# Output weights and bias centred on ScalarE, gamma applied by column groups, two plain loads on GpSimd's queue

## The chip, the cores and the metric

The kernel runs on one core of one Trainium2 chip. The metric is the device time of one launch in microseconds. The median of three runs of the kernel before is 727.76 us (727.09 to 733.88).

## The reference

The program is two graph networks behind each other on the same 384 nodes with 1024 features and 12,672 edges, each as a residual: `x = x + net(relu(layernorm(x)))`. The first is attention with an edge mask. The second is a relational graph convolution of two layers, 768 wide, with six relations and four basis matrices. Cut to what matters here:

```python
# second network, h is relu(layernorm(x)), 384 x 1024
x = relu(h @ w_in + b_in)                       # 384 x 768
for l in range(2):
    h_in = x
    W = einsum('rb,bio->rio', comp[l], basis[l])
    h_all = einsum('ni,rio->rno', x, W)
    counts = zeros((6, n)).at[edge_type, dst].add(1.0)
    msg = h_all[edge_type, src] / counts[edge_type, dst][:, None]
    agg = segment_sum(msg, dst, num_segments=n)
    x = relu(agg + x @ root[l] + conv_bias[l]) + h_in
    x = batchnorm(x, bn_gamma[l], bn_beta[l])
h_final = x @ w_out + b_out                     # 384 x 1024
out = ln_gamma * (h_final - mean) / sqrt(var + eps) + ln_beta   # mean, var over the 1024
```

The mean over the 1024 columns of `x @ w_out + b_out` is `x` times the row means of `w_out` plus the mean of `b_out`. If each row of `w_out` and `b_out` has its mean taken away, the product has mean zero.

## The kernel before, in words

Nodes or features lie on the 128 partitions; 384 nodes are three tiles. All products are in float32, and most large ones are made with seven partial products instead of eight (the functions that add and subtract quarters of an operand make the terms for this).

**The relation tables.** The edges are not followed one by one. GpSimd scatters edge counts into two tables in device memory, `atab[0]` and `atab[1]`, with 99 indirect transfers that add (`put_count`, line 269), in turns between the two tables; each waits for the one before it on the same table. The tables together give, for each relation, a 384 x 384 matrix of counts. When the scatters are done, the matrix of relation r is read into the tile `A[:, r]`: first a plain load of its part of table 1, then, from GpSimd's queue, a load of its part of table 0 that adds on arrival (line 836, `accum_op`). For relations 0 and 1 the plain load stands on SyncE's queue (line 834), for the other four on GpSimd's (line 838). `add_up` (lines 339 and 340, GpSimd) adds the three node tiles of a relation, `share` (line 345) sums over the partitions with a matmul against ones into a bank called `ps_cnt`, ScalarE and VectorE make one over the count from it (348 to 350), and VectorE scales the matrix (351). `mix` (330 and 332) then weighs the six relations into four matrices, one for each basis, in the tile `At`.

**The convolution.** For each layer the code runs over the four bases b. Each has three weight loads of 768 KB (`wload`, line 80, on SyncE's queue, from a pool of five buffers), products of the node features with the basis into `H` (lines 969 and 963, banks `ps_g`), and sums of weights on VectorE (911, 913, 919). The dictionary `between` puts the shares and mixes at fixed places between these products: share 0 after the first third of basis 2 of layer 0, share 1 after the second, share 2 after the last, share 3 and the first mix behind basis 2, shares 4 and 5 in basis 3, the other mixes behind basis 3. Then come the root product (1003) and the products of `At` with `H` (`times`, line 1061, banks `ps_c`), in three pairs of feature blocks o0 and o1. For each block VectorE adds a bank to `XN` (`take`, line 1091), ScalarE rectifies (`rectify`, 1094), VectorE adds the input and takes statistics (`measure`, 1026 to 1032), ScalarE takes a square root (1033), and VectorE scales (`normalise_layer`, 1038 to 1042). ScalarE has first put the root product with its bias into `XN` (`begin`, 1047).

**The output.** After the last layer the output weights stand in three tiles of [128, 2, 1024]. For each node tile TensorE makes the product (1167), VectorE adds the bias `rowsB[:, 0]` (1171), takes statistics by 256 columns (1173), joins them (145), adds epsilon (147), ScalarE takes the root (148), VectorE takes the mean away and multiplies by gamma `rowsB[:, 1]` in two halves (1178), takes the reciprocal (1179) and multiplies, adding `x_sb` (1181), and SyncE and ScalarE store the halves (1182). The last tile is cut in three groups of columns, 512, 256 and 256.

**What sets the order.** All engines around the change run in the order of the program's text: the schedule is manual for TensorE, GpSimd, SyncE and VectorE from the start and for ScalarE from the second projection on. An engine runs its instructions in that order and waits on semaphores, and a queue whose next transfer waits holds back those behind it.

Of the kernel before, what the change touches and what calls it, by code (L numbers as in the profile page):

```python
# [10 lines left out]
F32 = mybir.dt.float32  # L11
# [3 lines left out]
AF = mybir.ActivationFunctionType  # L15
ALU = mybir.AluOpType

P = 128
# [4 lines left out]
D = 1024  # L23
# [9 lines left out]
L = 2  # L33
# [18 lines left out]
def gnn_kernel(ctx: ExitStack, tc: tile.TileContext, out, x, edges, chunks, cols, rows, small,  # L52
               wq, wk, wv, wiq, wik, wiv, wo, w_in, basis, root, w_out):
    nc = tc.nc
# [7 lines left out]
    tiny = ctx.enter_context(tc.tile_pool(name="tiny", bufs=4))  # L62
# [4 lines left out]
    def bank(i, name):  # L67
        return psum.tile([P, 512], F32, tag=f"bank{i}", name=name)

    def next_bank(name, among=range(8)):  # L70

        i = next(i for i in ring if i in among)
        ring.remove(i)
        ring.append(i)
        return bank(i, name)

    def wload(src, name):

        w = wpool.tile([P, *src.shape[1:]], F32, tag="w", name=name)
        nc.sync.dma_start(w, src)  # L80
        return w
# [60 lines left out]
    def row_spread(st):  # L142

        mv = tiny.tile([P, 2], F32, tag="mv", name="mv")
        nc.vector.bn_aggr(mv, st.rearrange("p a b -> p (a b)"))
        sd = tiny.tile([P, 1], F32, tag="sd", name="sd")
        nc.vector.tensor_scalar(sd, mv[:, 1:2], LN_EPS, None, ALU.add)
        nc.scalar.activation(sd, sd, AF.Sqrt)
        return mv, sd
# [173 lines left out]
    A = None  # L323
# [32 lines left out]
    with ExitStack() as inner:  # L356
# [263 lines left out]
        A = late.tile([P, R, NT, N], F32, tag="A", name="A")  # L620
# [5 lines left out]
        scale = 1.0 / math.sqrt(HD)  # L626
# [164 lines left out]
        for half in range(2):  # L791
            T1, T2, T3, T4 = OT[half]
            pa, pb, pc, pd = [next_bank("ps_y", range(1, 8) if half else range(1, 7))[:, :256] for _ in range(4)]
            c0, c1 = half * 512, half * 512 + 256
# [36 lines left out]
        tabs = [tab[:ACELLS, :].rearrange("(t p r d) o -> r p t (d o)", p=P, r=R, t=NT) for tab in atab]  # L831

        for r in range(2):
            nc.sync.dma_start(A[:, r], tabs[1][r])
        for r in range(R):
            nc.gpsimd.dma_start(A[:, r], tabs[0][r], accum_op=ALU.add)
            for n in {1: (2, 3), 2: (4,), 3: (5,)}.get(r, ()):
# [52 lines left out]
    with tc.tile_pool(name="conv", bufs=1) as cp:  # L890
# [33 lines left out]
        def load_basis(l, b):  # L924
            w = w_first.pop(0) if w_first else []
            return w + [wload(basis[l, b, part], "w_c") for part in range(len(w), 3)]
# [20 lines left out]
        w = load_basis(0, 0)  # L947
        T = weight_sums(w)
        for l in range(L):
# [3 lines left out]
            for b in range(B):  # L953
# [6 lines left out]
                def times(ps, x, y, start=False):  # L960

                    for c in range(3):
                        nc.tensor.matmul(ps, x[:, c], y(c), start=start and c == 0, stop=(c == 2),  # L963
                                         skip_group_check=not start)
# [27 lines left out]
                if b + 1 < B:  # L992
                    w = load_basis(l, b + 1)
# [4 lines left out]
            w = [wload(root[l, part], "w_c") for part in range(3)]  # L998
# [11 lines left out]
            if l + 1 < L:  # L1010
# [4 lines left out]
                w = load_basis(l + 1, 0)  # L1015
            else:
# [3 lines left out]
                rowsB = room[:, :3 * D].rearrange("p (j d) -> p j d", j=3)  # L1020
# [15 lines left out]
            def normalise_layer(o, mv, sc):  # L1036
                c = l * KC + o
                nc.vector.reciprocal(sc[:, 0:1], sc[:, 0:1])
                nc.vector.tensor_tensor(sc[:, 1:2], sc[:, 0:1], cols_sb[:, GAM + c:GAM + c + 1], ALU.mult)
                nc.vector.tensor_tensor(sc[:, 2:3], mv[:, 0:1], sc[:, 1:2], ALU.mult)  # L1040
                nc.vector.tensor_tensor(sc[:, 2:3], cols_sb[:, BET + c:BET + c + 1], sc[:, 2:3], ALU.subtract)
                nc.vector.tensor_scalar(XN[:, o, :], XN[:, o, :], sc[:, 1:2], sc[:, 2:3], ALU.mult, ALU.add)

            def begin(o):

                c = l * KC + o
                nc.scalar.activation(XN[:, o, :], pr[o], AF.Identity, bias=cols_sb[:, CB + c:CB + c + 1])  # L1047
# [7 lines left out]
            def q(i, j):  # L1055

                return At.rearrange("p b n d -> p (b n) d")[:, i * 6:i * 6 + 6, j * HN:(j + 1) * HN]

            def times(ps, x, y, start=False, stop=True):
                for c in range(6):  # L1060
                    nc.tensor.matmul(ps, x[:, c], y[:, c], start=start and c == 0, stop=stop and c == 5,  # L1061
                                     skip_group_check=True)

            T1, T2 = [room2[:, i * 1152:(i + 1) * 1152].rearrange("p (c d) -> p c d", c=6) for i in range(2)]
            T4 = keep.tile([P, 6, HN], F32, tag="mask8", name="T4")
            nc.vector.tensor_tensor(T1, q(0, 1), q(0, 0), ALU.subtract)
# [6 lines left out]
            def feature_sums(p):  # L1073

                s0, s1, s3 = spaces[p % 2 * 3:][:3]
                o0, o1 = 2 * p, 2 * p + 1
                S.append((s0, s1, h(o1, 0), s3))
                for dst, x, y, op in ((s0, h(o1, 0), h(o1, 1), ALU.add), (s1, s0, h(o0, 0), ALU.subtract),
                                      (h(o1, 0), h(o0, 0), h(o1, 0), ALU.subtract),
                                      (s3, h(o0, 1), s1, ALU.subtract)):  # L1080
                    nc.vector.tensor_tensor(dst, x, y, op)
                    yield
# [6 lines left out]
            def take(o, j, ps):  # L1089
                dst = XN[:, o, j * HN:(j + 1) * HN]  # L1090
                nc.vector.tensor_tensor(dst, dst, ps, ALU.add)  # L1091
# [13 lines left out]
            for o in range(KC):  # L1105
                begin(o)
            take(0, 0, pa)
            ready = None
            for p in range(pairs):
                last = p == pairs - 1  # L1110
                sums = iter(()) if last else feature_sums(p + 1)
                o0, o1 = 2 * p, 2 * p + 1
                pc = next_bank("ps_c")[:, :HN]
                times(pc, S[p][0], T1, True)
                take(o1, 1, pc)
                if ready:
                    normalise_layer(*ready)
                next(sums, None)
                times(pa, S[p][1], T2)
                take(o0, 1, pa)  # L1120
                next(sums, None)
                times(pc, S[p][3], q(1, 1))
                take(o0, 1, pc)
                ready = measure(rectify(o0))
                if last:

                    pd = next_bank("ps_c")[:, :HN]
                    times(pd, h(o1, 1), T4, True)
                    normalise_layer(*ready)
                    take(o1, 0, pd)  # L1130
                    times(pa, S[p][2], T3)
                    take(o1, 1, pa)
                    take(o1, 0, pa)
                    normalise_layer(*measure(rectify(o1)))
                    continue
                times(pa, S[p][2], T3)
                take(o1, 1, pa)
                normalise_layer(*ready)
                for _ in sums:
                    pass  # L1140
                following = first_of(p + 1)
                times(pa, h(o1, 1), T4)
                take(o1, 0, pa)
                take(o1 + 1, 0, following)
                ready = measure(rectify(o1))
                pa = following
# [5 lines left out]

        for t in range(NT):
            nc.gpsimd.tensor_tensor(x_sb[:, t, :], x_sb[:, t, :], rowsB[:, 2, :], ALU.add)  # L1154
        w = [wload(w_out[part], "w_out") for part in range(3)]
        hf_ = cp.tile([P, NT, D], F32, tag="H", name="hf")
        for t in range(NT):
            hf = hf_[:, t, :]
            last = t == NT - 1
            ps = [next_bank("ps_f") for _ in range(3 if last else 2)]  # L1160

            parts = [(ps[0], 0, 512), (ps[1][:, :256], 512, 768), (ps[2][:, :256], 768, D)] if last else \
                [(ps[0], 0, 512), (ps[1], 512, D)]
            for ks in ((range(4), range(4, KC)) if t == 0 else (range(KC),)):
                for p, c0, c1 in parts:
                    for k in ks:
                        nc.tensor.matmul(p, XT[:, k, t * P:(t + 1) * P], w[k // 2][:, k % 2, c0:c1],  # L1167
                                         start=(k == 0), stop=(k == KC - 1))
            st = tiny.tile([P, 4, 6], F32, tag="st", name="st")
            for p, c0, c1 in parts:  # L1170
                nc.vector.tensor_tensor(hf[:, c0:c1], p, rowsB[:, 0, c0:c1], ALU.add)
                for c in range(c0, c1, 256):
                    nc.vector.bn_stats(st[:, c // 256, :], hf[:, c:c + 256])
            mv, sd = row_spread(st)

            parts = ((nc.sync, slice(0, 512)), (nc.scalar, slice(512, D)))
            for _, cs in parts:
                nc.vector.scalar_tensor_tensor(hf[:, cs], hf[:, cs], mv[:, 0:1], rowsB[:, 1, cs], ALU.subtract, ALU.mult)
            nc.vector.reciprocal(sd, sd)
            for queue, cs in parts:  # L1180
                nc.vector.scalar_tensor_tensor(hf[:, cs], hf[:, cs], sd, x_sb[:, t, cs], ALU.mult, ALU.add)
                queue.dma_start(out[t * P:(t + 1) * P, cs], hf[:, cs])
# [62 lines left out]
```

## Time and profile before

| | |
|---|---|
| median of three runs | 727.76 us |
| the profiled execution | 729.8 us, its span 728.0 us |
| TensorE busy | 700.2 us (96%) |
| VectorE busy | 515.0 us (71%) |
| GpSimd busy | 307.7 us (42%) |
| ScalarE busy | 157.7 us (22%) |
| mean granted TensorE clock | 0.991 |
| scatters into the count tables, line 269 | 99, 164.4 us busy |
| weight loads of a basis | 24 of 768 KB, 5.4 us from issue to landing in the median |
| relation loads on SyncE's queue, line 834 | 2 of 576 KB, 4.1 and 5.2 us to landing |
| relation loads on GpSimd's queue, lines 836 and 838 | 10 of 576 KB, 11.1 us to landing in the median |

All durations in the profile come from one execution, and the span is counted from the first instruction to the last. A line of a group gives busy time, the mean of one in nanoseconds, and the idle time before it with what ended it. In the timeline the first number is the start, the second the duration, and a bracket tells how long the engine had stood idle before and who released it. TensorE shows two records for each float32 matmul, so a group of six matmuls is x12.

### The profile page before, as it was taken

The numbers are of one execution on the slowest core, as the hardware profiler recorded it, in microseconds if no ns is written. First come the engines' busy times: TensorE is split into PE (matmuls) and PEld (weight loads), VectorE is DVE, ScalarE is ACT, GpSimd is POOL, SyncE is SP. The second block draws the span as 40 slices with busy tenths as digits, with TensorE's granted clock in tenths as the row PEclk, the third lists the DMA queues.
The fourth block names the chain that finished last, engine by engine and source line by source line (L and its number), as shares of the span: only waits on it lengthen the run. The fifth ranks groups of instructions, "written<-read, shape, count | busy, mean of one in ns | idle before, by whom it ended". The sixth has DMA issues, their size and how long they took to land.

```text
span 728.0 us, 8835 instructions
## 1 busy us (share of the span) xinstructions
PE 700.2 (96%) x3228; PEld 526.4 (72%) x3228; DVE 515.0 (71%) x1307; ACT 157.7 (22%) x360; POOL 307.7 (42%) x237
## 2 busy tenths in 40 slices
PE   7999999999999999999998499999999999999995
PEld 7759999999985444588965255557975555579943
DVE  6877696969877799777342179799878676506756
ACT  4201111111113577201310115201131111001100
POOL 1366677777575787586888454000000000030000
PEclk9999999999999999999999799999999999999999
DMA  8797787265426323525112997221103213700001
GB/s 300 261 364 206 235 248 216 43 218 198 126 71 207 84 3 61 169 33 131 1 2 0 251 319 208 85 89 44 43 1 131 76 59 125 277 27 1 1 29 58
DMA packets 40536, 91.00 MB, mean 125 GB/s; under 512 B 19644, under 2 KB 27680, under 8 KB 36270
## 3 DMA queue, kind: packets, MB, share of 16 engines
q1 hardware_dynamic: 18478, 79.62, 30.7%
q0 software_dynamic: 21008, 8.42, 10.1%
q10 hardware_dynamic: 1008, 2.41, 1.0%
q8 instruction: 25, 0.41, 0.2%
q14 instruction: 17, 0.14, 0.1%
HBM read 79.27 MB, written 11.16 MB: 124 GB/s over the span
## 4 chain that ended last, share of the span: by engine, by line
PE 60%; POOL 15%; DMA 10%; DVE 7%; issue 5%; ACT 1%; SPq 0%; DVEq 0%; POOLq 0%; ACTq 0%
POOL atab L269 14%; PE ps_k L386 10%; PE ps_g L969 10%; PE ps_c L1061 9%; PE ps_g L963 9%; DMA atab<-count,at 7%; PE ps_q L404 6%; PE ps_q L386 5%; PE ps_f L1167 4%; DVE At L332 4%; PE ps_v L386 4%; PE ps_c L1003 3%; DMA mtab<-m_val,at 2%; DMA w_c<-in_basis 1%; ACT At L330 1%
## 5 line engine op out<-in xcount | busy, mean ns | idle before, releaser
L269 POOL DMA_INDIRECT atab<-count,at x99 | 164.4, 1661 | 55.7 <-DMA atab<-count,at 29.3
L264 POOL DMA_INDIRECT mtab<-m_val,at x99 | 105.3, 1063 | 63.0 <-DMA mtab<-m_val,at 22.9
L1154 POOL TENSOR_TENSOR x_sb<-x_sb,room 128x1024 f32<-128x1024 f32 x3 | 7.0, 2355 | 188.4 <-DMA room<-in_rows 188.4
L969 PE MATMUL ps_g<-w_c,XT 128*128 128x384 f32 x144 | 50.0, 501 | 11.6 <-DMA w_c<-in_basis 11.6
L332 DVE SCALAR_TENSOR_TENSOR At<-A,small_sb,At 128x1152 f32<-128x1152 f32 x40 | 53.6, 1412 | 0.0
L969 PEld LDWEIGHTS ps_g<-w_c,XT 128*128 128x128 f32 x144 | 28.2, 197 | 31.7 <-DMA w_c<-in_basis 12.2
L963 PE MATMUL ps_g<-T,S 128*128 128x384 f32 x144 | 49.1, 486 | 0.0
L969 PE MATMUL ps_g<-w_c,XN 128*128 128x384 f32 x144 | 47.7, 487 | 1.1 <-DVE XN L1091 1.1
L404 PE MATMUL ps_q<-hT,w_q 128*128 128x384 f32 (+1 forms) x160 | 41.8, 422 | 1.4 <-ACT hT L90 1.4
L969 PEld LDWEIGHTS ps_g<-w_c,XN 128*128 128x128 f32 x144 | 27.3, 190 | 20.2 <-DVE XN L1091 1.4
L963 PEld LDWEIGHTS ps_g<-T,S 128*128 128x128 f32 x144 | 27.3, 190 | 19.2 <-ACT H L975 0.4
L404 PEld LDWEIGHTS ps_q<-hT,w_q 128*128 128x128 f32 x160 | 28.5, 190 | 14.1 <-ACT hT L90 1.6
L911 DVE TENSOR_TENSOR T<-w_c 128x768 f32<-128x768 f32 x24 | 24.5, 1022 | 17.7 <-DMA w_c<-in_basis 17.7
L1061 PE MATMUL ps_c<-At,H 128*128 128x192 f32 x216 | 36.4, 326 | 0.0
L1061 PEld LDWEIGHTS ps_c<-At,H 128*128 128x128 f32 x216 | 35.4, 190 | 0.5
L386 PE MATMUL ps_k<-T,S 128*128 128x192 f32 x192 | 35.1, 326 | 0.0
L1091 DVE TENSOR_TENSOR XN<-XN,ps_c 128x192 f32<-128x192 f32 x38 | 12.5, 348 | 30.9 <-ACT XN L1047 19.7
L386 PEld LDWEIGHTS ps_k<-T,S 128*128 128x128 f32 x192 | 31.9, 190 | 0.0
L1167 PE MATMUL ps_f<-w_out,XN 128*128 128x512 f32 (+1 forms) x84 | 31.1, 531 | 0.0
L659 DVE CUSTOM_DVE_ANT_0 s<-ps_s,mask 128x384 f32<-128x384 f32 x48 | 24.5, 549 | 5.3 <-PE ps_s L646 5.3
L253 DVE SCALAR_TENSOR_TENSOR same<-cells,own,later 128x128 f32<-128x128 int32 x99 | 27.9, 347 | 0.4
L253 DVE SCALAR_TENSOR_TENSOR same<-keys,key,weigh 128x128 f32<-128x128 int32 x99 | 27.8, 346 | 0.0
(297 smaller groups left out, 1403.2 us busy)
## 6 DMA issues: line engine op xcount, KB each, us to landing
w_c<-in_basis SPq DMA_DIRECT2D x24, 768.0 KB, 5.4
atab<-zero SPq DMA_DIRECT2D x12, 576.0 KB, 8.6
A<-atab POOLq DMA_DIRECT2D x10, 576.0 KB, 11.1
w_c<-in_root SPq DMA_DIRECT2D x6, 768.0 KB, 5.5
w_q<-in_wq SPq DMA_DIRECT2D x4, 1024.0 KB, 11.5
w_q<-in_wiq SPq DMA_DIRECT2D x4, 1024.0 KB, 13.6
w_k<-in_wk SPq DMA_DIRECT2D x4, 1024.0 KB, 6.5
w_k<-in_wik SPq DMA_DIRECT2D x4, 1024.0 KB, 6.1
```

The costliest lines, as they stand in the source:

```text
L253: nc.vector.scalar_tensor_tensor(same, row[:, n, :], mine[:, c:c + 1], times, ALU.is_equal, ALU.mult, accum_out=count[:, i, c:c + 1])
L264: nc.gpsimd.indirect_dma_start(mtab[c // PER][:, :], bass.IndirectOffsetOnAxis(at[:, 0, c:c + 1], 0), m_val[:, c:c + 1], None)
L269: nc.gpsimd.indirect_dma_start(atab[0 if i < 11 else i % 2][:, :], bass.IndirectOffsetOnAxis(at[:, 1, c:c + 1], 0), count[:, 1, c:c + 1], ...
L332: nc.vector.scalar_tensor_tensor(At[:, b], A[:, r], w, At[:, b], ALU.mult, ALU.add)
L386: nc.tensor.matmul(ps, a[:, k, :], b[:, k, :], start=start and k == 0, stop=(k == 3), skip_group_check=not start)
L404: nc.tensor.matmul(ps[o][:, c], wt_[:, k, o * P:(o + 1) * P], src[:, k, c], start=(k == 0 and c.start == 0), stop=(k == KD - 1 and c.stop ...
L659: nc.vector.tensor_tensor_reduce(s[j], ps[:, :N], mask8[:, t, :], -scale, 3.0e38, ALU.add, ALU.min, tops[:, j:j + 1])
L911: nc.vector.tensor_tensor(T13[:, c], w[c][:, :, HC:], w[c][:, 0, :].rearrange("p (o d) -> p o d", o=2), ALU.subtract)
L963: nc.tensor.matmul(ps, x[:, c], y(c), start=start and c == 0, stop=(c == 2), skip_group_check=not start)
L969: nc.tensor.matmul(ps, block(XT, n, i)[:, c], w[c][:, i, o * HC:(o + 1) * HC], start=(first and c == 0), stop=(c == 2 and (i == 1 or ps is ...
L1061: nc.tensor.matmul(ps, x[:, c], y[:, c], start=start and c == 0, stop=stop and c == 5, skip_group_check=True)
L1167: nc.tensor.matmul(p, XT[:, k, t * P:(t + 1) * P], w[k // 2][:, k % 2, c0:c1], start=(k == 0), stop=(k == KC - 1))
```

## The change

Three things are changed.

1. The two plain relation loads of line 834 are issued by GpSimd, not by SyncE.
2. In the last layer the three output weight loads are issued in the text before the pairs (they keep their place in SyncE's order, behind the root weights). ScalarE centres the bias row and then, at the head of each pair of feature blocks, the two rows of one weight tile: a pass with Identity that sums along the row into `mean`, a 128x1 pass that scales by -1/1024, and a pass with Identity that adds this as bias, all in place. The centrings of the bias and of the first tile stand in ScalarE's order after `begin` and before the first `rectify`; the second and third tile's stand between the square root of one pair's last block and the first `rectify` of the next pair.
3. In the output, the two passes that took the mean away and multiplied by gamma are gone. Gamma is multiplied by column groups, each right after its statistics; that of the last group of the last tile comes after `row_spread`. The mean of the statistics is no longer used.

```diff
         for r in range(2):
-            nc.sync.dma_start(A[:, r], tabs[1][r])
+            nc.gpsimd.dma_start(A[:, r], tabs[1][r])
...
+            def centre(row):
+
+                mean = tiny.tile([P, 1], F32, tag="mean", name="mean")
+                nc.scalar.activation(row, row, AF.Identity, accum_out=mean)
+                nc.scalar.activation(mean, mean, AF.Identity, scale=-1.0 / D)
+                nc.scalar.activation(row, row, AF.Identity, bias=mean)
...
             take(0, 0, pa)
+            if l + 1 == L:
+
+                w = [wload(w_out[part], "w_out") for part in range(3)]
+                centre(rowsB[:, 0, :])
             ready = None
             for p in range(pairs):
                 last = p == pairs - 1
                 sums = iter(()) if last else feature_sums(p + 1)
                 o0, o1 = 2 * p, 2 * p + 1
+                if l + 1 == L:
+                    for j in range(2):
+                        centre(w[p][:, j, :])
...
-        w = [wload(w_out[part], "w_out") for part in range(3)]
...
                 nc.vector.tensor_tensor(hf[:, c0:c1], p, rowsB[:, 0, c0:c1], ALU.add)
                 for c in range(c0, c1, 256):
                     nc.vector.bn_stats(st[:, c // 256, :], hf[:, c:c + 256])
+                if c1 < D or not last:
+                    nc.vector.tensor_tensor(hf[:, c0:c1], hf[:, c0:c1], rowsB[:, 1, c0:c1], ALU.mult)
             mv, sd = row_spread(st)
+            if last:
+                nc.vector.tensor_tensor(hf[:, c0:c1], hf[:, c0:c1], rowsB[:, 1, c0:c1], ALU.mult)

             parts = ((nc.sync, slice(0, 512)), (nc.scalar, slice(512, D)))
-            for _, cs in parts:
-                nc.vector.scalar_tensor_tensor(hf[:, cs], hf[:, cs], mv[:, 0:1], rowsB[:, 1, cs], ALU.subtract, ALU.mult)
             nc.vector.reciprocal(sd, sd)
```

## The prediction

> **What bounds the kernel now.** I read the page first: TensorE is busy 96% of the span, so time can come only from its few stalls, from the head and from the tail after its last matmul. The chain of work that ended last, asked for the stretch around 400 us, shows the one large stall (start, duration, what):
>
> ```profile
> 399.59 2.88 DMA atab<-count,at
> ...
> 402.49 0.38 SPq L834
> ...
> 403.56 6.43 DMA w_c<-in_basis
> 410.04 6.00 PE ps_g L969 x12
> ```
>
> The last scatter into the second relation table ends at 402.47, only then does SyncE's queue issue the two plain relation loads of line 834, and three weight loads that stood behind them follow. TensorE's wait and what it meets later stand in the timeline (start, duration, engine, line, operation, and in brackets its idle time and who ended it):
>
> ```profile
> 410.04 6.00 PE L969 MATMUL ps_g<-w_c,XT 128*128 128x384 f32 x12 [11.59 <-DMA w_c<-in_basis]
> ...
> 422.60 1.30 POOL L836 DMA_DIRECT2D A<-atab  x1 [3.22 <-DMA A<-atab]
> ...
> 425.80 1.60 POOL L340 TENSOR_TENSOR sum<-sum,A 128x384 f32<-128x384 f32 x1
> ...
> 429.42 0.81 PE L345 MATMUL ps_cnt<-sum,ones 128*128 128x384 f32 x2
> 433.94 0.81 PE L345 MATMUL ps_cnt<-sum,ones 128*128 128x384 f32 x2
> 434.10 1.00 POOL L340 TENSOR_TENSOR sum<-sum,A 128x384 f32<-128x384 f32 x1
> 438.45 0.81 PE L345 MATMUL ps_cnt<-sum,ones 128*128 128x384 f32 x2
> ```
>
> TensorE stood 11.59 us for a weight load, and its twelve records then took 6.00 us where the chain has 3.87 for the same group later; windows of 2 us give a granted clock of 0.50 from 404 to 412. The stall is thus worth 11.59 + 2.13 = 13.7 us. But behind it come the matmuls of line 345, one per relation, which need GpSimd's sums of line 340: the third sum ends at 435.1, its matmul starts at 438.45. So 3.35 us is all that can be gained while the sums stay where they are.
>
> **Part one: the two plain loads go to GpSimd's queue.** SyncE no longer waits at line 834. Its next three weight loads (last third of basis 1, two thirds of basis 2) need only the buffers of basis 0, whose last readers are the matmuls at 384.75; the same step one basis later (419.75) let SyncE issue at 420.59, so they start near 385.6, carry 3 x 768 KB, and land near 393, well before TensorE's need at 398.45. TensorE would begin basis 2 at 423.62 - 13.7 = 409.9 and stand before the first sum at 429.42 - 13.7 = 415.7. What is late then is the chain of sums, in four steps.
>
> First, the early loads meet the scatters, which set the time at which the tables may be read. Rows of such a meeting:
>
> ```profile
> 329.68 1.55 POOL L269 DMA_INDIRECT atab<-count,at  x1 [0.30 <-issue]
> 331.03 8.98 SPq L80 DMA_DIRECT2D w_c<-in_basis  x3
> 332.12 1.55 POOL L269 DMA_INDIRECT atab<-count,at  x1 [0.89 <-DMA atab<-count,at]
> 335.89 1.55 POOL L269 DMA_INDIRECT atab<-count,at  x1 [2.22 <-DMA atab<-count,at]
> 337.75 1.55 POOL L269 DMA_INDIRECT atab<-count,at  x1 [0.30 <-issue]
> ```
>
> Three undisturbed pitches of 1.855 are 5.57 us; here they took 8.07, so one load cost 2.5. The two loads after it (until 345.73) cost 2.4, the load at 307.48 cost 1.0 (305.52 to 312.02 against 5.57), and the burst of 3.9 MB at 287 cost 6.8 (288.34 to 298.85 against 3.7). For three loads of 2.36 MB I take 3.2, nearest to the rows of 768 KB, and keep 1.0 and 6.8 as ends. GpSimd is then free near 406.2, not 403.0, and issues the first plain load near 406.5.
>
> Second, three more weight loads, issued from 420.59 now, move by 13.7 to 406.9, beside it. How the two kinds of queue share is seen between 408 and 412: GpSimd's accumulating loads were issued at 407.37, yet the answer for that window lists only the other queue,
>
> ```profile
> q1 hardware_dynamic: 302, 1.66, 101.6%
> ```
>
> 302 packets, 1.66 MB, all engines full (415 GB/s). So the first plain load waits until the burst (5.7 us at that rate) is through near 414, moves its 0.59 MB in 1.5 us (396 GB/s in the window 420 to 422) and lands near 416.3. That is the choice on which most hangs. The Trainium skill, "DMA: Bandwidth & Descriptors", section "SWDGE vs HWDGE vs iDMA", says that each DMA engine alternates between the two kinds of queue, and that plain transfers belong on SyncE or ScalarE; this window shows no such alternation for 4 us. By the rule the first load would end with the burst, some 1.5 us earlier, and the forecast would be about 1.5 us lower.
>
> Third, the accumulating load follows at 416.5. Alone it takes 6.1 us from issue to use (issued 439.85, the add that needs it at 445.98): 422.6. The next plain load lands 4.9 later, 427.5 (5.3 now, 417.31 to 422.60, with a burst beginning in it).
>
> Fourth, from there to the end of the second sum is 4.8 us now (422.60 to 427.40), partly because VectorE ran beside it: 4.5, so 432.0. Then matmul 0.65 and the next third of basis 2, 3.87: the third share starts at 436.5, against 438.45. Its own sum, 427.5 + 6.1 + 2.1 = 435.7, isn't later. The remaining three sums have 7.4 us and more of room today (439.5 against 446.85 for the fourth) and go the same way. TensorE idles some 9 us before the first share, so its next third runs slow again (6.0), which its wait for the second sum hides: 424.7 + 0.65 + 6.0 is still under 432.0. **Part one: -2.0 us** of the 13.7. By the ends 1.0 and 6.8 it lies between -7 and +1: a delay over 3.2 mostly vanishes in the wait for the burst. VectorE's mixing (line 332, 26.6 us in the chain) starts after the last basis and keeps the gain.
>
> **Part two: centring on ScalarE, in the last layer.** Its rows are not in the trace, but near ones are: Identity over 128x1024 takes 1.24 us (line 436), reading an accumulator 0.19 with 0.1 showing (line 662), a 128x1 activation 0.20. One centring: 1.12 (without a bias, by the slope from 128x384 at 0.52 to 128x1152 at 1.24) + 0.1 + 0.2 + 1.24 + waits of 0.03 = 2.7 us; bounds 2.45 and 2.95. Seven of them are 19 us of ScalarE, 22% busy, but in its order they stand ahead of what the layer waits for:
>
> ```profile
> 662.73 0.52 ACT L1094 ACTIVATE XN<-XN 128x384 f32<-128x384 f32 x1 [5.25 <-DVE XN L1091]
> 663.29 0.56 DVE L1026 TENSOR_TENSOR XN<-XN 128x384 f32<-128x384 f32 x1 [0.65 <-ACT XN L1094]
> ...
> 664.77 0.34 DVE L1091 TENSOR_TENSOR XN<-XN,ps_c 128x192 f32<-128x192 f32 x1
> ...
> 665.98 2.11 PE L1061 MATMUL ps_c<-T,H 128*128 128x192 f32 x12
> ...
> 670.73 0.20 ACT L1033 ACTIVATE sc<-sc 128x1 f32<-128x1 f32 x1 [1.62 <-DVE sc L1032]
> ...
> 674.59 0.52 ACT L1094 ACTIVATE XN<-XN 128x384 f32<-128x384 f32 x1 [3.65 <-DVE XN L1091]
> ```
>
> Three centrings (bias and the first two columns) begin when the last line 1047 is over, 657.48, and end at 665.5; line 1094 wanted 662.73. Behind it VectorE waits in order at 663.29, and behind that the take at 664.77 that frees a PSUM bank, for which TensorE waits at 665.98: the take ends at 667.85, a stall of 1.9 us. In the second pair two centrings (5.3) follow the square root at 670.73, now 673.45, and end at 678.95; the chain asks 677.3 for line 1094. VectorE is then 4.4 late, and TensorE, at the same place (677.68 before), 3.7 in all. In the third pair line 1094 is 6.3 late, but only the output product waits for it: its fifth block would be wanted at 700.0 + 0.8 and the last normalisation ends at 694.31 + 6.3 = 700.6. So **+3.7 us**, from 2.5 to 5 by the bounds. The weights are on hand by 639.5, so no load is waited for.
>
> At the end, the two passes of line 1178 (1.40 us after the last statistics) become one 128x256 multiply of about 0.45; the other gammas go before, and VectorE has room (under 7 us of work in a 10.3 us period of TensorE). The reciprocal moves from 723.13 to 722.2: **-0.9 us**.
>
> **Sum.** -2.0 + 3.7 - 0.9 = +0.8 us against the profiled execution (729.8, its span 728.0 and 1.8 around). The median of the runs, 727.76, is 2.0 below that one, so I forecast 727.76 + 0.8 = 728.5 us. One per cent, 7.3 us, is about what can be told from no change.
>
> **Rivals.**
> - The plain loads slip in ahead of the burst. If the scatters lose only the 1.0 us of the row at 307, the first plain load is issued at 404.3 and lands at 409.3; the accumulating one ends with the burst, 418; the second sum 426.9, the third share 431.4: -7.0, in all -4.2: 723.5 us. For it: TensorE's own limit lies far off, 13.7. Against it: the rows at 331 and 339.
> - Slower: the chain of sums is the bound and gets later than now. If the plain load on GpSimd's queue takes 11.4 us, the median of its four on line 838, and each accumulating one 10.2, that of line 836: 406.5 + 11.4 + 10.2 + 4.9 = 433.0 for the third plain load, + 10.2 + 2.1 = 445.3 for the third sum, +6.9 on 438.45, in all +9.7: 737.4 us. It decides from 438.45 on, and passes 1% from a third share at 443. For it: these are the medians of GpSimd's own rows. Against it: those transfers stood behind each other and behind bursts.
> - ScalarE's work is hidden after all, because the shares of VectorE's slack are larger than I read: only -2.0 - 0.9, 724.9 us. Against it: VectorE shows no idle time between 666 and 669.
> - The early loads don't start early, because a buffer is held longer: the stall stays, the plain loads cost about 1 more, and with part two's +2.8 it is 731.6.
>
> **How the numbers follow.** Forecast 0.48, first rival 0.23, slower rival 0.15, hidden centring 0.10, late loads 0.04. The range leaves out the slower rival and the lowest corner: 722.5 to 734.5. Faster by over 1% (below 720.5) needs the first and third rival together, 0.06; slower by over 1% (above 735.0) is most of the slower rival, 0.14; within, 0.80.
>
> **What would show it.** Three weight loads near 386 and scatters stretched by about 3 us behind them; no stall at 398; instead a stall of some 9 us before the first line 345 and one before the second, both ended by GpSimd's sums; ScalarE without a gap from 652 to 665 and two TensorE stalls of 1.9 and 1.8 us in the last line 1061; one multiply after the last statistics. The forecast is wrong if the third share moves by more than 5 us either way, or if the two stalls at line 1061 miss.

## The result, and the profile after

The changed kernel takes 731.18 us in the median of 20 runs (727.29 to 737.87), the kernel before 730.05 us in the 20 runs beside it (725.22 to 738.29). The ratio is 1.0016, with a 95% interval of 0.9992 to 1.0040: no change that can be told. Here and below, a ratio leaves out executions that took over 1.5% more than the fastest of their kernel, and so can differ from the quotient of the two medians. The profiled execution has a span of 727.4 us, against 728.0.

The chain of work that ended last shows where the bound went. Its shares by engine after the change, with the line of the kernel before recalled in words:

```profile
PE 76%; DVE 10%; DMA 6%; ACT 4%; issue 2%; POOL 1%; another core or an unknown queue 1%; DVEq 0%; ACTq 0%; POOLq 0%
```

GpSimd, which had 15% of the chain before (its scatters up to the plain loads), has 1%. The same chain asked for the stretch around 400 us (start, duration, what):

```profile
398.47 6.39 DMA atab<-count,at
...
405.94 0.81 POOL A L834
406.75 6.14 DMA A<-atab
...
415.10 8.03 DMA A<-atab
...
423.42 9.80 DMA A<-atab
...
433.30 1.69 POOL sum L339
...
435.05 1.00 POOL sum L340
```

The weight load that carried the chain in the kernel before (6.43 us of `w_c<-in_basis`) is gone; the relation loads and GpSimd's sums carry it now, up to the third share. The timeline of the same stretch:

```profile
396.35 22.90 SPq L80 DMA_DIRECT2D w_c<-in_basis  x6
...
404.96 1.55 POOL L269 DMA_INDIRECT atab<-count,at  x1 [4.93 <-DMA atab<-count,at]
405.19 7.90 PE L969 MATMUL ps_g<-w_c,XT 128*128 128x384 f32 x24
405.94 2.24 POOL L834 DMA_DIRECT2D A<-atab  x2
411.45 1.31 POOL L836 DMA_DIRECT2D A<-atab  x1 [3.27 <-DMA A<-atab]
...
426.48 0.81 PE L345 MATMUL ps_cnt<-sum,ones 128*128 128x384 f32 x2
...
435.05 0.99 POOL L340 TENSOR_TENSOR sum<-sum,A 128x384 f32<-128x384 f32 x1
...
436.10 0.91 PE L345 MATMUL ps_cnt<-sum,ones 128*128 128x384 f32 x2 [0.43 <-POOL sum L340]
```

Three things are to be seen. TensorE has no wait for weights in this stretch. The last scatter was issued after an idle time of 4.93 us behind three early weight loads. And the third share starts at 436.10 (438.45 before), held by the third sum for 0.43 us. What these rows don't show is that TensorE came into this stretch late: its first instruction of line 680 (a transpose in the attention) starts at 243.67 us in the profile before and at 254.52 here, 10.85 us later, in code that no part of the change touches. "Late" is meant so from here on. So the vanished wait is not the change's work alone, and the experiments below had to find out how much of it is.

In the last layer ScalarE's new work stands in the timeline as forecast, three centrings without a gap and then what the layer waits for:

```profile
660.06 1.04 ACT L1067 ACTIVATE w_out<-w_out 128x1024 f32<-128x1024 f32 x1
...
661.01 0.19 ACT L1067 ACTIVATION_READ_ACCUMULATOR w_out<-w_out 128x1 f32 x1
661.22 0.20 ACT L1068 ACTIVATE mean<-mean 128x1 f32<-128x1 f32 x1
661.46 1.15 ACT L1069 ACTIVATE w_out<-w_out,mean 128x1024 f32<-128x1024 f32 x1
...
663.05 0.56 DVE L1026 TENSOR_TENSOR XN<-XN 128x384 f32<-128x384 f32 x1 [2.65 <-ACT XN L1101]
...
664.93 2.22 PE L1061 MATMUL ps_c<-T,H 128*128 128x192 f32 x12 [1.02 <-DVE XN L1098]
...
677.76 2.22 PE L1061 MATMUL ps_c<-T,H 128*128 128x192 f32 x12 [0.58 <-DVE XN L1098]
```

VectorE waited 2.65 us for ScalarE, and TensorE 1.02 and, in the second pair, 0.58 us for the take that frees a bank. (After the change the take is line 1098, the rectification 1101.) At the end one multiply follows the last statistics:

```profile
721.98 0.42 DVE L1191 TENSOR_TENSOR hf<-hf,room 128x256 f32<-128x256 f32 x1
...
722.33 0.16 DVE L1194 RECIPROCAL sd<-sd 128x1 f32<-128x1 f32 x1
```

The reciprocal started at 723.13 before. TensorE begins the output product (line 1180, 1167 before) at 689.56 here and at 689.38 before, so the way from there to the reciprocal is 0.98 us shorter.

### The profile page after: what moved, and what is told of

The parts are those of the page before. It is cut to its first block, busy times and chain, and to the rows that moved or that the text cites. A ratio compares the mean times of both kernels' runs of the same rounds, so it can differ in the third digit from the quotient of the medians.

```text
span 727.4 us, 8859 instructions
## 1 busy us (share of the span) xinstructions
PE 701.9 (97%) x3228; PEld 527.8 (73%) x3228; DVE 514.8 (71%) x1308; ACT 173.8 (24%) x388; POOL 307.9 (42%) x239
## 4 chain that ended last, share of the span: by engine, by line
PE 76%; DVE 10%; DMA 6%; ACT 4%; issue 2%; POOL 1%; another core or an unknown queue 1%; DVEq 0%; ACTq 0%; POOLq 0%
PE ps_k L386 10%; PE ps_v L386 8%; PE ps_g L969 7%; PE ps_g L963 7%; PE ps_c L1061 7%; PE ps_q L404 6%; PE ps_q L386 5%; PE ps_f L1180 4%; DVE At L332 4%; PE ps_y L386 3%; DMA A<-atab 3%; PE ps_c L1003 3%; PE ps_x L386 3%; PE ps_o L691 2%; PE ps_s L646 2%; PE ps_pT L680 2%
## 5 line engine op out<-in xcount | busy, mean ns | idle before, releaser
L969 PE MATMUL ps_g<-w_c,XT 128*128 128x384 f32 x144 | 47.9, 486 | 0.0
L386 PE MATMUL ps_k<-T,S 128*128 128x192 f32 x192 | 36.7, 336 | 8.4 <-ACT k L502 5.8
L1180 PE MATMUL ps_f<-w_out,XN 128*128 128x512 f32 (+1 forms) x84 | 31.1, 531 | 0.0
L1180 PEld LDWEIGHTS ps_f<-w_out,XN 128*128 128x128 f32 x84 | 15.9, 190 | 14.9 <-issue 14.3
```

The source lines that it names most:

```text
L386: nc.tensor.matmul(ps, a[:, k, :], b[:, k, :], start=start and k == 0, stop=(k == 3), skip_group_check=not start)
L969: nc.tensor.matmul(ps, block(XT, n, i)[:, c], w[c][:, i, o * HC:(o + 1) * HC], start=(first and c == 0), stop=(c == 2 and (i == 1 or ps is ...
```

## The experiments

The theory to be tested was the forecast's sum: the plain loads gain 2.0 us, since the chain of GpSimd's sums is the next bound; the centrings cost 3.7 us through their place in ScalarE's order; the tail gains 0.9. The rivals were a gain of 7 us from the loads, a loss of up to 7 us through the sums, and centrings that are hidden. "Ratio" is against runs of the kernel before on the same chip, with its 95% interval.

**The loads alone.**

```diff
-            nc.sync.dma_start(A[:, r], tabs[1][r])
+            nc.gpsimd.dma_start(A[:, r], tabs[1][r])
```

> The kernel before with one line changed: the two plain relation loads on GpSimd's queue. Theory (the stall behind SyncE's wait goes, but the relation sums then bound the shares): about -2.0 us, ratio 0.997; no TensorE stall for a basis load; instead one of up to 9 us before the first share and small ones before the second and third, ended by GpSimd's sums; the third share starts near 436.5 against 438.45. Rival one (the changed kernel lost its stall only because TensorE came 10.8 us late in that execution, by a wait at 140 us): 0 us, the stall is still there when TensorE is on time. Rival two (plain loads in front of the burst): -7 us, third share near 431.

Measured: 733.3 us (728.21 to 751.04) against 732.99, ratio 1.0056 (1.0009 to 1.0103). No gain; a loss stands in the ratio, but not in the medians of all runs. TensorE came 16.4 us late into the stretch; no wait for a sum is seen, and the third share started at 441.06.

**The centring and gamma alone** (the changed kernel with line 834 back on SyncE).

```diff
-            nc.gpsimd.dma_start(A[:, r], tabs[1][r])
+            nc.sync.dma_start(A[:, r], tabs[1][r])
```

> The changed kernel with the two plain relation loads back on SyncE: centring and gamma alone. By the prediction's terms +3.7 - 0.9 = +2.8 us, ratio 1.004. By the trace of the changed kernel, where one centring took 2.45 us and not 2.7 and TensorE lost 2.4, +2.4 - 1.0 = +1.4 us, ratio 1.002; two TensorE stalls in the last line 1061, of about 1.0 to 1.9 us each. Rival (ScalarE's work is hidden): -0.9 us, no such stalls. The 11.6 us stall for a basis load is back in every case.

Measured: 732.21 us, ratio 1.0016 (0.9968 to 1.0065), too wide to tell 2.8 us from nothing. The profile tells more: the last line 1061 lost 2.4 us, as in the changed kernel. And the loads stood on SyncE, yet TensorE had no wait for weights, where the stall of 11.6 us was expected back; it came 17.6 us late. The stall of the forecast is not a fixture of the kernel before.

**The centrings where ScalarE is free.** All seven are put ahead of `begin` in the text, with the loads of the output weights.

```diff
+            if l + 1 == L:
+                w = [wload(w_out[part], "w_out") for part in range(3)]
+                for p in range(pairs):
+                    for j in range(2):
+                        centre(w[p][:, j, :])
+                    if p == 1:
+                        centre(rowsB[:, 0, :])
...
-                w = [wload(w_out[part], "w_out") for part in range(3)]
-                centre(rowsB[:, 0, :])
...
-                    for j in range(2):
-                        centre(w[p][:, j, :])
```

> The changed kernel with all seven centrings moved in ScalarE's order ahead of the six begin instructions (line 1047), where ScalarE waits 22.8 us for the products. Theory (the cost of part two is ScalarE's place in the order, not its amount): the two stalls in the last line 1061 go, 2.4 us less than the changed kernel; against before -2.3 - 1.0 = -3.3 us, ratio 0.9955. Rival (centring costs by something else, such as a slower product with weights just written): no better than the changed kernel, ratio about 1.001.

Measured: 734.25 us, ratio 1.0036 (0.9989 to 1.0084). TensorE has no wait in the last line 1061 any more, so the price of the centrings is that of their place. The 3.3 us that were expected don't show in the time. The profiled execution lost more at the relations; its timeline there:

```profile
396.65 22.90 SPq L80 DMA_DIRECT2D w_c<-in_basis  x6
...
405.52 1.56 POOL L269 DMA_INDIRECT atab<-count,at  x1 [5.37 <-DMA atab<-count,at]
...
432.19 1.65 PE L345 MATMUL ps_cnt<-sum,ones 128*128 128x384 f32 x2 [5.25 <-POOL sum L340]
```

Early weight loads held a scatter for 5.37 us, the first plain load was issued only at 412.91, and the first share waited 5.25 us for its sum: the slower rival's mechanism, in one execution. The third share started at 444.65.

**The loads stay on SyncE, but behind the next weights.** The block that loads the relations is called from `load_basis`, behind two thirds of basis 2.

```diff
+        def load_relations():
             for r in range(2):
                 nc.sync.dma_start(A[:, r], tabs[1][r])
...
+            for part in range(len(w), 3):
+                if (l, b, part) == (0, 2, 2):
+                    load_relations()
+                w.append(wload(basis[l, b, part], "w_c"))
```

> The kernel before with the whole block of relation loads moved in the text behind two thirds of basis 2, so that on SyncE's queue the two plain loads stand behind three more weight loads but stay on that queue. Theory (the sums' chain is the bound, and the queue of the plain loads counts): no stall for a basis load; the plain loads land 4 to 5 us after the last scatter and not 5.5, and the next weight burst stands behind them: third share near 434, -4 us, ratio 0.9945. Rival (the queue doesn't matter, the scatters stretched by the early weight loads do): the same as with GpSimd's queue, -2 us.

Measured: 731.78 us, ratio 1.0031 (0.9993 to 1.0070). Neither the 4 us of the theory nor the rival's 2 us were gained. With the plain loads on SyncE's queue, too, a scatter behind early weight loads was held up, by about as much as in the profiles above, and here the second share waited for its sum (the third started at 443.77):

```profile
397.35 1.62 SPq L80 DMA_DIRECT2D w_c<-in_basis  x3
...
406.41 1.55 POOL L269 DMA_INDIRECT atab<-count,at  x1 [5.49 <-DMA atab<-count,at]
...
436.12 1.65 PE L345 MATMUL ps_cnt<-sum,ones 128*128 128x384 f32 x2 [3.97 <-POOL sum L340]
```

**Both kernels again, and the centrings early without moved loads.** The last is the third experiment's kernel with this edit:

```diff
-            nc.gpsimd.dma_start(A[:, r], tabs[1][r])
+            nc.sync.dma_start(A[:, r], tabs[1][r])
```

> The kernel before, unchanged, once more. It tells how much of the first profile was that one execution. Theory (in four of four later profiles TensorE is 11 to 17 us later at 200 us than in the profile of before, by waits at 100 to 200 us that no edit touches): its profile too shows TensorE some 11 us or more late at 200 us, and the stall for a basis load is then under 3 us or gone. Rival (the edits cause that lateness): TensorE is on time, and the stall of 11.6 us is there. Ratio 1.000, with an interval that tells the noise.

> The changed kernel, unchanged, once more. Theory: TensorE late by 11 us or more at 200 us; two stalls in the last line 1061 of about 1.0 and 1.1 us in sum; if the three weight loads start before the last scatters, one scatter waits about 5 us; ratio 1.000 to 1.003. Rival (part one gains 2 us whatever TensorE does): ratio 0.998 or less.

> The kernel before with centring ahead of the begin instructions and gamma by column groups; the relation loads stay on SyncE's queue. Theory (part one is worth nothing in most executions, part two's cost is ScalarE's order alone): the tail's gain of 0.96 us is left, ratio 0.9987, no TensorE stall in the last line 1061. Rival (part one gains 2 us): this is 2 us slower than the same with the loads moved.

Measured: the kernel before 730.85 us, ratio 0.9992 (0.9960 to 1.0024) against itself; the changed one 731.09, 1.0011 (0.9982 to 1.0040); early centrings with the loads on SyncE 729.43, 0.9997 (0.9962 to 1.0031). The last has the shortest span of these, 725.9 us, but its times don't tell it from the kernel before. The second profile of the kernel before does show the stall again, smaller:

```profile
414.47 6.36 PE L969 MATMUL ps_g<-w_c,XT 128*128 128x384 f32 x12 [8.17 <-DMA w_c<-in_basis]
```

TensorE was 7.8 us late in that execution, and the third share started at 443.24, not at 438.45.

**TensorE later by 14.2 us.** The kernel before with 64 matmuls that nobody uses, ahead of layer 0's bases.

```diff
+        ps = bank(ring[0], "ps_late")
+        for _ in range(64):
+            nc.tensor.matmul(ps[:, :P], ones, ones, start=True, stop=True)
```

> The kernel before with 64 matmuls of 128x128 (about 14 us) that nothing uses put on TensorE ahead of basis 0 of layer 0. It measures how much room TensorE has before the wait for the basis load. Theory (TensorE usually comes 11 us or more late of itself and the stall is mostly gone): about +11 to +14 us, ratio 1.015 to 1.019. Rival (the 13.7 us stall is there in most executions): the added work fills it, +1 us, ratio 1.001.

Measured: 742.39 us, ratio 1.0145 (1.0077 to 1.0212), which is 10.6 us (0.0145 of 730.8; 5.6 to 15.5 by the interval of only four runs). If the usual execution had a stall of 13.7 us, the extra work would nearly vanish in it. About 3.6 of the 14.2 us do, at most 8.6 by the interval.

**TensorE earlier by 9.0 us**, first with the loads on SyncE, then on GpSimd's queue, and the loads alone once more.

```diff
-                    for c in range(3):
+                    cs = range(3) if (l, b) != (0, 0) else range(1)
+                    for c in cs:
...
+                        if (l, b, c) == (0, 0, 1):
+                            continue
                         nc.tensor.matmul(ps, block(XT, n, i)[:, c], w[c][:, i, o * HC:(o + 1) * HC],
```

> The kernel before, with part of basis 0 of layer 0 left out (the middle third of line 969's products, and two of three steps of four of the five combined products, so the output isn't the reference's): TensorE has some 9.0 us less to do (12 records of 3.87 us together, and 4 times 1.29) ahead of the place where it may wait for the weights behind the relation loads. If that wait is mostly absent because TensorE is usually late, it comes back here, at about the place of the first profile (TensorE at about 399, the weights at about 410), and of the 9.0 us only 3 to 6 are gained: a time of 724 to 727. If the wait is there in a usual execution already, TensorE just waits longer and nearly nothing is gained: within 1.5 us of the kernel before.

> The same as the run before, with the two plain relation loads on GpSimd's queue: the condition under which the change's first part was forecast. The forecast of part one (a weight wait of 11 us gone, but the chain of GpSimd's sums next in line) gives a third share 2.0 us earlier and a time 2.0 lower than the run before (7 lower to 1 higher). With the stretch of about 5 us seen in the scatters (not 3.2) the first plain load issues near 406 and the chain of sums gains nothing: the first and second share wait 5 us or more for a sum, and the time is within 1.5 us of the run before.

> The kernel before with only the two plain loads on GpSimd's queue, a second time, beside five rounds of the kernel before. If the 1.0056 of the first time (1.0009 to 1.0103) was the spread of the executions, the ratio is within 0.2% of 1; if moving the loads costs a usual execution something, it is again above 1.003.

Measured: with the loads on SyncE 729.69 us (726.21 to 733.91), ratio 1.0014 (0.9983 to 1.0044); on GpSimd's queue 733.73 (725.05 to 749.93), 1.0034 (0.9994 to 1.0074); the loads alone 733.01 (727.55 to 743.55), 1.0010 (0.9970 to 1.0050). The kernel before took 732.54 us beside them. Nine microseconds of TensorE's work taken away gained nothing by the ratio, and 2.9 us by the medians of all runs. The first of these profiles shows where they went, into a longer wait for weights:

```profile
412.51 5.96 PE L972 MATMUL ps_g<-w_c,XT 128*128 128x384 f32 x12 [17.48 <-DMA w_c<-in_basis]
```

Its third share is at 440.88. In this condition, for which the forecast's part one was worked out, the moved loads bring no gain in the time either: 0.2% more, with intervals that overlap. In the profiles of the other two TensorE was 24 to 27 us late, so only their times are used. The loss of 0.56% for the loads alone wasn't repeated.

**Why TensorE is late.** In the late executions the lost time lies in the projections between 85 and 195 us, as waits for ScalarE, which in turn waits for something that the trace doesn't name. The changed kernel's timeline:

```profile
141.77 0.42 ACT L498 ACTIVATE k<-ps_k,cols_sb 128x192 f32<-128x192 f32 x1 [8.95 <-remote]
142.24 1.57 PE L386 MATMUL ps_k<-T,S 128*128 128x192 f32 x8 [2.60 <-issue]
...
150.90 1.33 PE L386 MATMUL ps_k<-T,S 128*128 128x192 f32 x3 [5.79 <-ACT k L502]
```

GpSimd scatters the edge mask just then (line 264, 61 of its 99 transfers between 85 and 200 us). The last experiment leaves these scatters out.

```diff
             for r in range(*PIECES[p:p + 2]):
-                for j in range(tables_in(r)):
-                    put_mask(j * PER + r)
                 if r in DEALT:
```

> The kernel before with the 99 indirect transfers of line 264 left out, which scatter the edge mask from GpSimd's queue while the projections run (so the attention mask is incomplete and the output isn't the reference's); the 99 scatters of line 269 stay. In most profiles TensorE arrives at 200 us some 10 to 25 us later than in the first profile of before, through waits in the projections between 85 and 195 us. If the traffic of the mask scatters brings these waits about, TensorE's time at line 386 near 200 us is within 2 us of the first profile, and the executions lie closer together than the 25 us (724.55 to 750.09) of the kernel before in the last series, with a median 3 or more us lower. If the waits come from elsewhere, TensorE is again 5 to 25 us late in the profile and the executions spread as widely as those of the kernel before.

Measured: 715.94 us, six runs within 715.75 to 717.49, against 731.8 (723.79 to 736.35, 11 runs); ratio 0.9806 (0.9766 to 0.9846). The spread shrinks from 12.6 to 1.7 us. Groups of the stretch from 85 to 200 us, the changed kernel (busy, mean ns | idle time ahead and what ended it):

```profile
L386 PE MATMUL ps_k<-T,S 128*128 128x192 f32 x192 | 36.7, 336 | 8.4 <-ACT k L502 5.8 <-issue 2.6
```

and without the mask scatters (two lines higher in the code):

```profile
L384 PE MATMUL ps_k<-T,S 128*128 128x192 f32 x192 | 35.1, 326 | 0.0
```

The waits are gone. But this row alone shows little, since the first profile of before, with the mask scatters, has no waits there either:

```profile
L386 PE MATMUL ps_k<-T,S 128*128 128x192 f32 x192 | 35.1, 326 | 0.0
```

What carries the reading is that all six runs are short and alike, where the kernel before is now on time and now late. The stall for weights is gone too, since GpSimd is through with its count scatters some 36 us sooner (the last is issued at 365.04, not at 401.44). This run therefore takes away two things at once: that the late executions come with the mask scatters is shown; by which path a scatter holds ScalarE up is not, and stays open. Its span is 715.7 us against 728.0, and its third share starts at 426.13 against 438.45: both 12.3 us earlier. TensorE is 1.45 us late here, and the two together are the 13.7 us at which the forecast put the stall of that execution.

## Why the prediction was right or wrong

The total was right: 0.8 us more was forecast, the ratio says 0.16%, about 1.2 us, with an interval that holds both the forecast and zero. The 731.18 us stand 2.7 above the forecast 728.5, mostly because the kernel before took 730.05 us in 20 runs and 727.76 in the first three. Taken term by term, one was right, one had the right mechanism and the wrong size, and one rested on a premise that doesn't hold.

**The tail, -0.9 us: right.** It measured -0.98 up to the reciprocal.

**The centring, +3.7 us: the mechanism right, the size too large.** Three centrings ahead of the first rectification, two behind the square root, VectorE late, TensorE waiting at two places of the last line 1061: all of it is in the trace. One centring took 2.45 us, the lower bound of the estimate, not 2.7: the summing pass 1.04, the accumulator 0.19, the mean 0.20, the last pass 1.15 where 1.24 was taken from line 436, the rest small overlaps and gaps. Five centrings, each 0.25 us shorter, make up nearly all of the difference. The waits came to 1.0 and 0.6 and the whole to 2.4 us in three profiles (the changed kernel, its repeat, the centring alone), since matmuls behind a wait were slower too, 2.22 us for a group and not 2.11. It is counted from the first product of the last layer that reads `room` (656.23 before, 653.99 here) to the output product, 33.15 us before and 35.57 here. "Hidden after all" is refuted by these waits, and the two kernels with early centrings, at 33.15 again, show that the place in ScalarE's order is the cause.

**The plain loads, -2.0 us: some steps held, the premise failed.** What is left of the measured 1.2 us after +2.4 and -1.0 is an estimate of -0.3 us for this term; the interval leaves -2 to +1.5, so these times alone don't exclude the forecast. Forecast were scatters stretched by 3.2 us, the first plain load issued near 406.5, a third sum at 435.7, a third share at 436.5. The changed kernel's profile has one idle time of 4.93 us, the issue at 405.94, the third sum done at 436.04 and the share at 436.10. The stalls of TensorE before the first and second share didn't come: they started without a wait, the first at 426.48. The stretch was mis-sized: idle times of 4.9 to 5.5 us, against 0.30 undisturbed, in three profiles where early weight loads met scatters still to come.

The plain load itself was quicker than forecast, landing about 411.4 and not 416.3 (of which 0.8 have no source in the forecast's sum: 414 and 1.5 make 415.5), because the next weight burst wasn't beside it: TensorE was late and hadn't freed the buffers, and SyncE issued that burst only at 417.64. So how a plain load shares with a burst was not put to the test there. The scatters did share: between 399 and 404 us the changed kernel's trace has 356 packets of SyncE's queue and 230 of GpSimd's. The fourth rival, weight loads that start late, is refuted: they were issued at 396.35, which is, within 0.1 us, the forecast's 385.6 and the 10.85 by which TensorE was late.

But the numbers agree partly by luck. The forecast let TensorE arrive at 398.45, as in the one profile that it had, and then counted a gain against 438.45, the third share of that execution. In the later profiles of the two kernels and of mixtures of their parts, that share started between 437.24 and 443.24 with line 834 on SyncE, and between 436.10 and 448.73 with the loads moved. Nor do the times show a gain: the loads alone measured 1.0056 and 1.0010, and with TensorE made early 1.0034 against 1.0014. So the step that failed is "SyncE no longer waits at line 834, TensorE would begin basis 2 at 409.9, and the share moves from 438.45": from execution to execution TensorE's arrival varies by 10 us or more, through waits far ahead of the stretch.

That the queue makes no difference where TensorE comes late enough can be read from the profiles directly. This is TensorE's way from its first instruction of line 680 to the third share (us), in profiles without a wait for weights or sums:

| profile | plain loads on | line 680 | third share | between |
|---|---|---|---|---|
| centring alone | SyncE | 261.30 | 442.29 | 180.99 |
| early centrings | SyncE | 256.07 | 437.24 | 181.17 |
| no mask scatters | SyncE | 245.12 | 426.13 | 181.01 |
| changed kernel again | GpSimd | 255.70 | 436.70 | 181.00 |
| loads alone | GpSimd | 260.10 | 441.06 | 180.96 |

The first profile of before has 194.78, 13.8 us more: the stall was sized rightly, for that execution.

Why the loads gain nothing in an early execution is seen less directly. Taking 9.0 us off TensorE gains nothing by the ratio (its interval allows 1.2 us at most, 0.0017 of 732), and adding 14.2 us costs 10.6. The kernel before stands about where TensorE's arrival and the end of the scatters meet. When TensorE is early, the tables are what it waits for, with the weights as the messenger; moving the plain loads to another queue makes no table ready sooner, and lets weight loads through that hold the last scatters up by 5 us. Counted from the issue of the last scatter, the third share came 37.0, 37.7 and 37.3 us later with the loads on SyncE (before, before again, TensorE early), and 31.1 and 33.6 with the loads moved (the changed kernel, early centrings): the 3.5 to 6.5 us gained there are about what that scatter had lost. This rests on two profiles with moved loads. When TensorE is late, there is no stall to remove. The first rival (7 us gained) is refuted by the times; the slower rival's mechanism was seen in one profile with moved loads, the first share waiting 5.25 us for a sum, but the times show no loss of its size.

## What to carry to other kernels

Before a stall of one profile is booked as a gain, ask whether the arrival of the waiting engine is the same in every execution: a spread of 6.8 us among three runs of an unchanged kernel was the warning here, and adding or removing known work ahead of the stall told what it was worth. To compare profiles of a program whose executions differ, measure between two places of one engine: 181.0 us told more here than the clock times. Follow a wait back to what is produced last, not to the queue that delivers it; letting other transfers pass the blocked one can slow the producer. A small job given to an idle engine costs by its place in that engine's order, so put it where nothing behind it is waited for.

## What the runs showed of the hardware that was not expected

- Waits of ScalarE at the evictions of the projections, differing from execution to execution of a program on one core (8.95 us idle ahead of line 498 in the changed kernel, where the first profile of before has 4.8 on average, 38.3 over 8), moved TensorE by 5 to 18 us at line 680. Without the 99 indirect mask transfers they were absent, and the times of six runs lay within 1.7 us.
- Behind three 768 KB weight loads on SyncE's queue the next indirect transfer of GpSimd's queue was issued after an idle time of 4.93, 5.37 and 5.49 us; undisturbed, after 0.30 us.
- A plain 576 KB load on GpSimd's queue took 5.5 us from issue to the instruction behind it (405.94 to 411.45), not the 11 us that the rows of the kernel before had as their median, where loads stood behind each other.
- On ScalarE a 128x1024 pass took 1.04 us with a sum along the row and 1.15 us with a bias from each partition.
